# Attention's projections and layer 0's gate and up products: seven float32 products of sums, or three float32r passes over split operands

## The chip, the cores and the metric

The kernel runs on one core of a Trainium2 chip. The metric is the device time of one execution in microseconds (us), as the median of several runs; lower is better. The profile speaks of engines: PE is TensorE's matrix products and PEld its weight loads, DVE is VectorE, ACT is ScalarE, POOL is GpSimd, and SP is the engine that issues most of the transfers. [...]

## What is computed

Two transformer layers over 4 sequences of 256 tokens with 256 features, float32, with a layer norm after each of four sublayers:

```python
x = layernorm(x + L0_attn(x))   # 16 heads, 128 plain + 64 rotary features each, values of 128
x = layernorm(x + L0_ffn(x))    # silu(x W1^T) * (x W3^T), a Walsh-Hadamard transform, W2
x = layernorm(x + L1_attn(x))   # mLSTM with 8 heads, then a gated MLP of its own
x = layernorm(x + L1_ffn(x))    # gated MLP with int8 weights and scales

# L0_attn
q, k, v = x @ Wq.T, x @ Wk.T, x @ Wv.T
scores = q_nope k_nope / sqrt(128) + rope(q_rope) rope(k_rope) / sqrt(64)
out = (softmax(scores) @ v).reshape(...) @ Wo.T
```

## The kernel before

**Blocks of attention.** Heads are taken by pairs p (8 pairs), tokens by halves n (512 tokens, two sequences). One block h = 2p + n holds the scores and softmax of pair p and half n, and three other things that fill TensorE meanwhile: the projections of block h + 1, the weighted values of block h - 1 (steps V00 to V11), and the output products of block h - 1 (O0, O1), which are added to `acc[n]`. There are 16 blocks. The order of TensorE's instructions in a block is written out by hand (`ORDER`, and `EARLY` for the first two); `in_turn` chains each product behind the last. All engines run their own instructions strictly in the built order; what stands on VectorE, GpSimd or the transfer queue behind a waiting instruction waits too. `behind(x)` makes an instruction come after x.

**Scores and softmax.** `scores` makes the plain products (L455) into four PSUM banks, two with the tag `sc` and two with `pt`, and the rotary ones (L467) on top. `maxima` (L478, DVE), `exponentials` (L487, ACT), `normalized` (L495 and L497, DVE) and `block_transposed` (L505, DVE) follow for each sequence and head; `finish(k)` is normalisation and block transposition of one of the four. `spread` (L512) then completes the transposition with 16 transfers from SP's queue into `prT`, and the next block's V steps wait for all of these.

**Projections.** For the first block they are plain float32 products (`projections`). For the others `fast_projections` uses a Winograd form of Strassen's scheme: each pair of 2x2 blocks (256 input features in two halves, 512 tokens in two sequences) takes seven products of sums of blocks instead of eight. The sums of the weights (`weight_sums`, L285 to L288, DVE) are made once a pair, those of the input (`input_sums`) once a half. There are four groups: rotary (3), plain queries (0), plain keys (1), values (2); steps A1 to A7 take groups 3 and 0 in banks `mm`, steps B1 to B7 groups 1 and 2 in banks `sc`. Rotary products are scaled, added, then turned: `turn` exchanges neighbouring partitions (`stream_shuffle`, L312, DVE) and GpSimd multiplies by cosine and sine and adds (L315 to L317, three instructions of 128x512 for queries and three for keys). The shuffle of blocks after the first is held behind the last normalisation of the softmax:

```python
with behind(settled["softmax"]) if h > 1 else contextlib.nullcontext():
    nc.vector.stream_shuffle(swp, raw[c], SWAP)
```

**PSUM.** A tag is a ring of two banks of 512 columns: `mm`, `sc`, `pt`, `ot`. A product that starts a bank waits until the bank's last reader is done.

**Layer 0's feed-forward.** `ffn0(0)` uses the same seven products (`fast_glu`), `ffn0(1)` plain float32 products of 512 columns (`glu`). The Walsh-Hadamard transform is folded into W2: butterflies on GpSimd (L678, L679) during attention, and four products with `had` (L687), two in the last block and two ahead of the feed-forward. `ffn0(1)` is interleaved with mLSTM of half 0 by `merge`, which gives the second stream so many us of TensorE work for each wait of the first; so it goes on with `ffn1(0)` and mLSTM of half 1. Layer norms and RMS norms (`layernorm`, `rmsnorm`, with `rsqrt` in 13 small DVE instructions) are taken over four token tiles at a time.

**Layer 1's feed-forward** already uses float32r: a float32 input is split into a rounded part and the rest, and each meets the int8 weights, which need no splitting, in one product of one pass (L1279 with 512 columns, L1329 with 256).

Of the kernel before, what the change touches and what calls it, by code (L numbers as in the profile page):

```python
# [17 lines left out]
P = 128  # L18
# [17 lines left out]
SWAP = [i ^ 1 for i in range(32)]  # L36


@with_exitstack
def tile_two_layers(ctx: ExitStack, tc: tile.TileContext, a: dict, out: bass.AP):  # L40
# [10 lines left out]
    def rsqrt(v, n, scale, eps):  # L51

        ve = small.tile([P, n], F32, tag="rs_v", name="rs_v")
        nc.vector.tensor_scalar(ve, v, scale, eps, ALU.mult, ALU.add)
        sh = small.tile([P, n], I32, tag="rs_sh", name="rs_sh")
# [20 lines left out]
    xT = attn.tile([P, KC, NT], F32, tag="xT", name="xT", bufs=1)  # L76
# [16 lines left out]
    def load_pair(p):  # L93

        w = attn.tile([P, KC, 3 * 384], F32, tag="w", name="w_qkv", bufs=2)
        if p == 0:
            for i in range(KC):
                nc.sync.dma_start(w[:, i, 0:256], a["w_qkv"][p][:, i, 0:256])
            for lo, hi in ((256, 384), (640, 768), (384, 640)):
                nc.sync.dma_start(w[:, :, lo:hi], a["w_qkv"][p][:, :, lo:hi])  # L100
            load_tables()
            nc.sync.dma_start(w[:, :, 768:1024], a["w_qkv"][p][:, :, 768:])
            nc.sync.dma_start(cst[:, 512:1024], a["cst"][:, 640:1152])
        else:
            nc.sync.dma_start(w[:, :, 0:1024], a["w_qkv"][p])
        wr = attn.tile([P, KC, 2, P], F32, tag="wr", name="w_rot")
        if p != 1:
            turned_weights(w, wr)
        return w, wr

    def turned_weights(w, wr):

        for i in range(KC):
            for k in range(2):
                nc.gpsimd.tensor_copy(
                    wr[:, i, k, :].rearrange("p (h f x) -> p h f x", h=2, x=2),
                    w[:, i, 256 + 384 * k : 384 + 384 * k].rearrange("p (h x f) -> p h f x", h=2, x=2),
                )

# [7 lines left out]
    weights = {0: load_pair(0)}  # L127
    nc.sync.dma_start(xT[:, :, HALF:], a["xT"][:, :, HALF:])
# [5 lines left out]
    weights[1], w_os[1] = load_pair(1), load_output(1)  # L134
# [4 lines left out]
    def ff_weight(name, engine=nc.sync, dtype=F32):  # L139

        tiled = [P, NH, D] if name in ("w2", "w_down", "q_down") else [P, KC, FF]
        t = wts.tile(tiled, dtype, tag="ff", name=name, bufs=7)
# [4 lines left out]
    pair_sums = lambda k: wts.tile([P, 4, 4 * P], F32, tag="ff", name=f"wsum{k}", bufs=7)  # L147
    wsums = [pair_sums(0)]
    xsum = wts.tile([P, 2, 4, S], F32, tag="ff", name="xsum", bufs=7)
    wsums.append(pair_sums(1))  # L150
    w2b = wts.tile([P, NH, D], F32, tag="ff", name="w2b", bufs=7)
    w2, w1, w3 = (ff_weight(k) for k in ("w2", "w1", "w3"))

# [11 lines left out]
    def hidden_sums(engine, ws, which, to=None):  # L165


        for x, w in enumerate(ws):
            part = lambda i, c: w[:, i, :].rearrange("p (k c d) -> p k c d", c=2, d=P)[:, :, c, :]
            one, two = gsum[:, 0, x], gsum[:, 1, x]  # L170
            if which == "first":
                engine.tensor_tensor(one, part(0, 1), part(1, 1), ALU.add)
                last = engine.tensor_tensor(two, one, part(0, 0), ALU.subtract)
            elif which == "third":
                last = engine.tensor_tensor(gsum3[:, x], part(0, 0), part(0, 1), ALU.subtract)
            else:
                last = engine.tensor_tensor(to[:, x] if to else part(0, 1), part(1, 0), two, ALU.subtract)
        return last

    def projections(h):  # L180
# [3 lines left out]
        w, wr = weights[p]  # L184
# [80 lines left out]
    def input_sums(n):  # L265
        tok = lambda b: slice((2 * n + b) * S, (2 * n + b + 1) * S)
        one, two, three, four = (xsum[:, n, m, :] for m in range(4))
        nc.vector.tensor_tensor(one, xT[:, 0, tok(1)], xT[:, 0, tok(0)], ALU.subtract)
        nc.vector.tensor_tensor(two, xT[:, 1, tok(1)], one, ALU.subtract)
        nc.vector.tensor_tensor(three, xT[:, 1, tok(1)], xT[:, 0, tok(1)], ALU.subtract)  # L270
        return nc.vector.tensor_tensor(four, xT[:, 1, tok(0)], two, ALU.subtract)

    def weight_sums(p, groups=((0, 3), (3, 4))):


        w, wr = weights[p]
        sums = wsums[p % 2]
        for g0, g1 in groups:
            if g0 == 3:
                part = lambda i, c: wr[:, i, c, :]  # L280
                at = lambda m: sums[:, m, 384:512]
            else:
                part = lambda i, c: w[:, i, :].rearrange("p (g c x) -> p g c x", g=3, c=3)[:, g0:g1, c, :]
                at = lambda m: sums[:, m, 0:384].rearrange("p (g x) -> p g x", g=3)[:, g0:g1, :]
            nc.vector.tensor_tensor(at(0), part(0, 1), part(1, 1), ALU.add)  # L285
            nc.vector.tensor_tensor(at(1), at(0), part(0, 0), ALU.subtract)
            nc.vector.tensor_tensor(at(2), part(0, 0), part(0, 1), ALU.subtract)
            last = nc.vector.tensor_tensor(at(3), part(1, 0), at(1), ALU.subtract)  # L288
        return last

    def fast_projections(h):

        p, n = divmod(h, 2)
        w, wr = weights[p]
# [5 lines left out]
        batch = lambda b: slice(b * S, (b + 1) * S)  # L300
        raw = []

        def rotary(c, b):
            if not raw:
                raw.extend(attn.tile([P, HALF], F32, tag="raw", name="rope_raw", bufs=3) for _ in range(2))
            return raw[c][:, batch(b)]

        def turn(c):

            swp = attn.tile([P, HALF], F32, tag="swp", name="rope_swp", bufs=3)  # L310
            with behind(settled["softmax"]) if h > 1 else contextlib.nullcontext():
                nc.vector.stream_shuffle(swp, raw[c], SWAP)  # L312
            by_b = lambda t: t.rearrange("p (b s) -> p b s", s=S)
            cs, sn = (t.unsqueeze(1).to_broadcast([P, 2, S]) for t in (cos, sin))
            nc.gpsimd.tensor_tensor(by_b(raw[c]), by_b(raw[c]), cs, ALU.mult)  # L315
            nc.gpsimd.tensor_tensor(by_b(swp), by_b(swp), sn, ALU.mult)  # L316
            rotated[h] = nc.gpsimd.tensor_tensor((qr, kr)[c], raw[c], swp, ALU.add)  # L317

        def group(which):

            at = (0, 384, 768, None)[which]
            if which == 3:
                block = lambda c, i: wr[:, i, c, :]
            else:
                block = lambda c, i: w[:, i, at + c * P : at + (c + 1) * P]
            dst = (
                lambda c, b: qn[:, c, batch(b)],
                lambda c, b: kn[:, c, batch(b)],
                lambda c, b: v[:, 2 * b : 2 * b + 2, c * P : (c + 1) * P],
                rotary,  # L330
            )[which]
            scales = ((QSCALE, QSCALE), (1.0, 1.0), (1.0, 1.0), (RSCALE, 1.0))[which]
            return which, block, dst, scales

        def factors(g, m):
            which, block = g[0], g[1]
# [13 lines left out]
        def pair_of_groups(tag, which):  # L350
# [3 lines left out]
            def products(name, m, start):  # L354
                if start and name not in found:
                    found[name] = bank(tag)
# [1049 lines left out]
    for c in (2, 3):  # L1406
        hadamard(c)
# [135 lines left out]
```

## Time and profile before

| | |
|---|---|
| Runs (us) | 694.88, 694.0, 696.69; median 694.88 |
| Profiled execution: span | 692.4 us from the first to the last instruction; its own time is not listed apart from the runs, whose median is 2.5 us above the span |
| Engines busy | PE 680.3 us (98%), DVE 474.0 (68%), ACT 280.2 (40%), POOL 183.0 (26%) |
| Granted TensorE clock | 0.997 of full speed |
| Attention blocks 2 to 14 | start 24.68 us apart, at 63.0 to 383.8 us |
| Layer 0's feed-forward, first half | products from 410 to 437 us |
| Layer 1's int8 feed-forward | from 638 us to the end |

A row of the profile names the line, the engine, the operation, the tile written and the tiles read, and the shape. In a group, "busy" is the sum, then comes the mean of one in ns. In a timeline, the first two numbers are start and duration in us, "x8" merges eight instructions in a row, and a bracket tells how long the engine had been idle and who released it. One float32 product appears as two PE records. Records of PE include the pipeline's fill and drain, so the time that a product takes of TensorE is the distance from start to start.

### The profile page before, as it was taken

To read this page: it belongs to the slowest core of one execution; us is meant where nothing else is said; L and a number is where in the kernel's file an instruction comes from. 1 tells how busy PE (TensorE), PEld (TensorE's weight loads), DVE (VectorE), ACT (ScalarE), POOL (GpSimd) and SP (SyncE) were. 2 spreads that over 40 slices of the span, in tenths; PEclk is the share of its full clock that TensorE was granted. 3 is DMA by queue.
4 is the path that set the end of the run, shared out by engine and by line. 5 is a ranking of instruction groups with operands and counts; after the bars stand their busy time and mean duration, and the time that the engine had idled before them with its cause. 6 is when DMAs were issued, how large, how long until landed. Compare 5 with 4: busy or idle time off the path is not lost.

```text
span 692.4 us, 10218 instructions
## 1 busy us (share of the span) xinstructions
PE 680.3 (98%) x3504; PEld 551.4 (80%) x3504; DVE 474.0 (68%) x1310; ACT 280.2 (40%) x839; POOL 183.0 (26%) x191
## 2 busy tenths in 40 slices
PE   9999999999999999999999999999999999999995
PEld 5888988988888898898888878845685568788785
DVE  5966766666477478467747786474779648966767
ACT  2442543344254254334425355136412561261652
POOL 3254314413431440441442920004100140000210
PEclk9999999999999999999999999999999999999998
DMA  8543233232331421520331322003031300001001
GB/s 270 216 123 61 39 100 62 54 95 51 67 96 36 108 66 26 138 57 17 64 62 28 96 47 87 1 0 124 1 121 62 120 4 1 0 1 62 0 1 62
DMA packets 49030, 45.46 MB, mean 66 GB/s; under 512 B 9521, under 2 KB 42705, under 8 KB 47825
## 3 DMA queue, kind: packets, MB, share of 16 engines
q1 hardware_dynamic: 48112, 41.00, 22.8%
q0 software_dynamic: 432, 3.15, 1.3%
q10 hardware_dynamic: 432, 0.66, 0.3%
q8 instruction: 28, 0.46, 0.3%
q14 instruction: 26, 0.20, 0.1%
HBM read 25.61 MB, written 1.08 MB: 39 GB/s over the span
## 4 chain that ended last, share of the span: by engine, by line
PE 88%; DVE 8%; ACT 2%; POOL 1%; issue 1%; DVEq 0%; ACTq 0%
PE ps_mm L371 13%; PE ps_mm L70 10%; PE ps_ot L70 8%; PE ps_d L70 7%; PE ps_sc L363 6%; PE ps_sc L371 6%; PE ps_d L930 4%; PE ps_d L1279 4%; PE ps_m L70 4%; PE ps_sc L455 4%; PE ps_pt L455 4%; PE ps_m L871 4%; PE ps_d L871 3%; PE ps_sc L467 2%; PE ps_m L930 2%; PE ps_m L1195 2%
## 5 line engine op out<-in xcount | busy, mean ns | idle before, releaser
L315 POOL TENSOR_TENSOR rope_raw<-rope_raw,cst 128x512 f32<-128x512 f32 x30 | 38.2, 1272 | 181.8 <-DVE rope_swp L312 181.8
L487 ACT ACTIVATE pr<-ps_sc,nmax 128x256 f32<-128x256 f32 x64 | 29.7, 475 | 121.3 <-DVE nmax L478 121.3
L70 PE MATMUL ps_mm<-w_o,oT 128*128 128x256 f32 x256 | 62.2, 379 | 0.0
L70 PE MATMUL ps_ot<-prT,v 128*128 128x256 f32 x240 | 61.4, 380 | 0.1
L569 DVE TENSOR_TENSOR acc<-ps_mm,acc 128x512 f32<-128x512 f32 x32 | 22.1, 690 | 48.3 <-PE ps_mm L70 48.3
L70 PEld LDWEIGHTS ps_mm<-w_o,oT 128*128 128x128 f32 x256 | 46.6, 190 | 5.3
L70 PEld LDWEIGHTS ps_ot<-prT,v 128*128 128x128 f32 x240 | 43.3, 190 | 5.5 <-issue 0.8
L1153 POOL TENSOR_TENSOR ex<-cst,ex 128x512 f32<-128x512 f32 x16 | 19.7, 1266 | 93.7 <-DMA ex<-far 93.7
L385 ACT COPY kn<-ps_sc 128x256 f32<-128x256 f32 x56 | 20.9, 373 | 58.3 <-PE ps_sc L363 58.2
L497 DVE TENSOR_SCALAR pr<-pr,rinv 128x256 f32<-128x256 f32 x128 | 42.8, 375 | 1.6
L371 PE MATMUL ps_mm<-xsum,wsum 128*128 128x256 f32 x180 | 43.9, 380 | 0.0
L505 DVE STREAM_TRANSPOSE cross<-pr 128x512 f32<-128x512 f32 x60 | 42.6, 711 | 1.4
L478 DVE TENSOR_REDUCE nmax<-ps_sc 128x2 f32<-128x512 f32 x32 | 20.6, 686 | 32.7 <-PE ps_sc L467 32.6
L316 POOL TENSOR_TENSOR rope_swp<-rope_swp,cst 128x512 f32<-128x512 f32 x30 | 38.1, 1270 | 0.0
L371 PEld LDWEIGHTS ps_mm<-xsum,wsum 128*128 128x128 f32 x180 | 33.9, 190 | 4.5
L394 DVE TENSOR_TENSOR kn<-ps_sc,kn 128x256 f32<-128x256 f32 x42 | 17.8, 423 | 28.5 <-ACT kn L385 18.1
L487 ACT ACTIVATE pr<-ps_pt,nmax 128x256 f32<-128x256 f32 x64 | 30.1, 489 | 2.6 <-DVE nmax L478 2.6
L455 PE MATMUL ps_sc<-kn,qn 128*128 128x256 f32 x128 | 30.2, 379 | 0.0
L455 PE MATMUL ps_pt<-kn,qn 128*128 128x256 f32 x128 | 30.2, 379 | 0.0
L70 PE MATMUL ps_d<-fm,w 128*128 128x512 f32 x64 | 29.4, 599 | 0.0
L930 PE MATMUL ps_d<-w,hT 128*128 128x256 f32 x128 | 28.4, 379 | 0.0
L363 PEld LDWEIGHTS ps_sc<-wsum,xsum 128*128 128x128 f32 x168 | 25.4, 191 | 2.2
(317 smaller groups left out, 1631.0 us busy)
## 6 DMA issues: line engine op xcount, KB each, us to landing
prT<-cross SPq DMA_DIRECT2D x240, 64.0 KB, 2.1
w_qkv<-in_w_qkv SPq DMA_DIRECT2D x7, 1024.0 KB, 7.0
ex<-far SPq DMA_DIRECT2D x8, 512.0 KB, 5.1
w<-in_w SPq DMA_DIRECT2D x3, 1024.0 KB, 11.6
w_o<-in_w_o SPq DMA_DIRECT2D x8, 256.0 KB, 3.3
acc<-in_x SPq DMA_DIRECT2D x2, 512.0 KB, 9.0
w_up<-in_w_up SPq DMA_DIRECT2D x1, 1024.0 KB, 4.9
w_gate<-in_w_gate SPq DMA_DIRECT2D x1, 1024.0 KB
```

The source lines that it names most:

```text
L70: last = nc.tensor.matmul(ps, lhsT=lhs(i), rhs=rhs(i), start=(i == 0), stop=(i == n - 1))
L315: nc.gpsimd.tensor_tensor(by_b(raw[c]), by_b(raw[c]), cs, ALU.mult)
L316: nc.gpsimd.tensor_tensor(by_b(swp), by_b(swp), sn, ALU.mult)
L363: lambda: nc.tensor.matmul(ps[:, k * S + j * P : k * S + (j + 1) * P], lhsT=x[:, j * P : (j + 1) * P], rhs=wt, start=(start and not k and ...
L371: lambda: nc.tensor.matmul(ps[:, k * S : (k + 1) * S], lhsT=wt, rhs=x, start=(start and not k), stop=True, skip_group_check=True,)
L455: lambda: nc.tensor.matmul(ps[bb][e][:, qt * S : (qt + 1) * S], lhsT=qn[:, e, queries(bb, qt)], rhs=kn[:, e, keys(bb)], start=(qt == 0), s ...
L487: nc.scalar.activation(pr[:, qt, :], ps[:, qt * S : (qt + 1) * S], AF.Exp, bias=nmax[:, qt : qt + 1], accum_out=rsum[:, qt : qt + 1],)
L497: nc.vector.tensor_scalar(pr[:, qt, :], pr[:, qt, :], rinv[:, qt : qt + 1], None, ALU.mult)
L505: return nc.vector.transpose(cross[:, :, e], pr.rearrange("p t (x i) -> p x t i", i=32))
L871: nc.tensor.matmul(banks[name][:, batch(x)], lhsT=left, rhs=right, start=start and not x, stop=True, skip_group_check=True,)
L930: lambda: nc.tensor.matmul(po, lhsT=hT[:, i, j * P : (j + 1) * P], rhs=wd[:, i, :], start=(i == 0), stop=(i == NH - 1),)
L1279: nc.tensor.matmul(ps, lhsT=lhs, rhs=rhs, start=(k == 0), stop=(k == len(terms) - 1))
```

## The change

**Three passes.** Each float32 operand of the projections is written as the sum of a high part of 12 significant bits (the low 12 bits masked off) and the rest. With high parts H, h and rests L, l, the product is found from three one-pass float32r products of prepared operands, with the scale 2^-12 (`STEP`): two kinds are summed in one PSUM bank, the third in another, and a result is bank 0 times (1 + 2^-12), minus bank 1. So each group of 128 output features takes 6 products of 512 columns and fills two banks; ScalarE copies the first with the scale, VectorE subtracts the second (`joined`). Values take 24 products of 256 columns a block. `ffn0` uses the same for both halves (`split_glu`, 12 products of 512 columns for each pair of gate and up tiles).

**Splitting.** `split` masks on DVE, subtracts on POOL (or DVE for inputs), joins mask and rest on DVE, and copies on ACT. A pair's weights have four parts, R (rotary), Q, K and W (values), split one pair ahead: R, Q and K in even blocks after steps Q0, K0 and W0, W in odd blocks after R1. `weight_sums`, `input_sums` and the Strassen sums of layer 0's feed-forward go.

**Order.** The blocks have a new `ORDER`; the rotary groups come first, in banks `mm` and `sc`, and the shuffle is no longer held behind the softmax. Blocks 0 and 1 use `ot` in place of `sc`.

**Memory and loads.** The parts, the Strassen sums that stay (layer 1's MLP, half 1), and the feed-forward weights share named slots; one buffer instead of two takes a pair's raw weights; w1 and w3 are loaded near the end of attention and split there (`hidden_parts`); w_gate and w_up load after layer 0's gate and up. The Hadamard products move into blocks 12 and 13. Layer 1's int8 parts lie in quarters.

**Norms by pairs.** The norm ahead of mLSTM is joined with the layer norm before it, from the same statistics, for two token tiles at a time right after their rows are done (`mlstm_rows`); the norm ahead of layer 1's MLP goes by pairs too (`mlp_rows`). The waits that `merge` is given change with it.

The diff, cut to its core:

```diff
-            nc.sync.dma_start(w[:, :, 0:1024], a["w_qkv"][p])
+            nc.sync.dma_start(w, a["w_qkv"][p])          # bufs=1 instead of 2
...
+    def split(src, to, top, scaled, engine=nc.gpsimd, views=None, fine=nc.vector):
+        if views is None:
+            views = [(src, top, to[1])]
+        for x, t, low in views:
+            nc.vector.tensor_single_scalar(t.bitcast(I32), x.bitcast(I32), TOP, ALU.bitwise_and)
+        for x, t, low in views:
+            engine.tensor_tensor(low, x, t, ALU.subtract)
+        low = to[1].bitcast(F32)
+        if scaled:
+            nc.scalar.mul(to[1], low, 1.0 / STEP)
+            last = nc.vector.tensor_tensor(to[2], top, low, ALU.subtract)
+        elif fine is nc.gpsimd:
+            nc.scalar.mul(to[2], top, STEP)
+            last = nc.gpsimd.tensor_tensor(to[2], to[2].bitcast(F32), low, ALU.subtract)
+        else:
+            last = nc.vector.scalar_tensor_tensor(to[2], top, STEP, low, ALU.mult, ALU.subtract)
+        nc.scalar.copy(to[0], top)
+        return last
...
+        def passes(ps, left, right, first=True):
+            for at, ks in ((0, (0, 1)), (1, (2,))):
+                terms = [(k, i) for i in range(KC) for k in ks]
+                for m, (k, i) in enumerate(terms):
+                    in_turn(lambda: nc.tensor.matmul(ps[at], lhsT=left(k, i), rhs=right(k, i), ...))
+        def joined(dst, ps, scale):
+            copied = nc.scalar.mul(dst, ps[0], scale * (1.0 + STEP))
+            if scale == 1.0:
+                return copied, nc.vector.tensor_tensor(dst, dst, ps[1], ALU.subtract)
+            return copied, nc.vector.scalar_tensor_tensor(dst, ps[1], -scale, dst, ALU.mult, ALU.add)
...
-            with behind(settled["softmax"]) if h > 1 else contextlib.nullcontext():
-                nc.vector.stream_shuffle(swp, raw[c], SWAP)
+            nc.vector.stream_shuffle(swp, raw, SWAP)
...
-    ORDER = "A1 A2 V00 A6 V01 A7 A5 B1 B2 A3 A4 B6 B7 V10 B5 V11 O0 B3 O0 B4 O1 O1".split()
+    ORDER = "R0 V00 V01 R1 V10 Q0 V11 O0 O0 Q1 K0 K1 O1 O1 W0 W1".split()
+    SPLITS = ({"Q0": "R", "K0": "Q", "W0": "K"}, {"R1": "W"})
...
+            elif step == "R1":
+                with behind(done):
+                    finish(1)
+                with behind(copied):
+                    found.append(exponentials(ps[1][1], top[3]))
+            elif step == "Q0":
+                with behind(done):
+                    finish(2)
+            elif step == "Q1":
+                with behind(done):
+                    settled["softmax"] = finish(3)
                 out = spread(crossed)
+            name, ahead = SPLITS[h % 2].get(step), h // 2 + 1
+            if name and ahead < NPAIR:
+                with behind(settled["softmax"] if step[0] in "KW" else done):
+                    pair_part(ahead, name)
...
+    def split_glu(x, wg, wu, hT, tag, smooth):
+        for c in range(NH):
+            pg, pu = [bank(tag) for _ in range(2)], [bank(tag) for _ in range(2)]
+            fill(lambda: three_products(pg, wg, x, c))
+            yield 1.35
+            fill(lambda: three_products(pu, wu, x, c))
...
+    def mlstm_rows(n, j):
+        ...
+        nc.vector.tensor_scalar(ve[:, 0:2], mv[:, :, 1], 1.0 + RMS_EPS, RMS_EPS * LN_EPS, ALU.mult, ALU.add)
+        nc.vector.tensor_scalar(ve[:, 2:4], mv[:, :, 1], LN_EPS, None, ALU.add)
+        y = root(ve, 4)
```

## The prediction

> **What bounds the kernel now.** First the page: how busy each engine is, and which engine carries the chain that ended last.
>
> ```profile
> PE 680.3 (98%) x3504; PEld 551.4 (80%) x3504; DVE 474.0 (68%) x1310; ACT 280.2 (40%) x839; POOL 183.0 (26%) x191
> ...
> PE 88%; DVE 8%; ACT 2%; POOL 1%; issue 1%; DVEq 0%; ACTq 0%
> ```
>
> TensorE is the bound over nearly the whole span. Second, the table by stretches, for 13 equal attention blocks, 63.0 to 383.8 us (columns: length, then busy us of PE, PEld, DVE, ACT, POOL):
>
> ```profile
> 63.00:383.80 320.80, 320.80 (x1743) 280.92 (x1742) 213.65 (x546) 130.40 (x442) 106.62 (x102) 1.00 0.29 64
> ```
>
> A block takes 320.8 / 13 = 24.68 us, VectorE works 16.4 us of it, GpSimd 8.2. Third, the chain in order of time through one block shows no engine but PE, so nothing but TensorE work sets a block's length:
>
> ```profile
> 309.94 1.73 PE ps_sc L455 x8
> 311.66 1.73 PE ps_pt L455 x8
> 313.39 1.06 PE ps_sc L467 x8
> 314.45 0.86 PE ps_pt L467 x8
> 315.32 0.84 PE ps_mm L371 x3
> ```
>
> Fourth, the timeline, for what a float32r product costs and for what VectorE and GpSimd do to each other:
>
> ```profile
> 649.31 1.07 PE L1279 MATMUL ps_d<-qx,q_gate 128*128 128x512 f32 x4
> 650.22 1.07 PE L1279 MATMUL ps_d<-qx,q_up 128*128 128x512 f32 x4
> ...
> 673.12 11.67 PE L1329 MATMUL ps_m<-q_down,qh 128*128 128x256 f32 x96
> ```
> ```profile
> 14.46 1.46 POOL L205 TENSOR_TENSOR rope_raw<-rope_raw,cst 128x512 f32<-128x512 f32 x1
> 15.88 1.44 POOL L207 TENSOR_TENSOR qr<-rope_raw,rope_swp 128x512 f32<-128x512 f32 x1
> ```
> ```profile
> 14.72 1.48 DVE L270 TENSOR_TENSOR xsum<-xT 128x256 f32<-128x256 f32 x1
> 16.12 1.48 DVE L269 TENSOR_TENSOR xsum<-xT,xsum 128x256 f32<-128x256 f32 x1
> ...
> 299.87 0.35 DVE L497 TENSOR_SCALAR pr<-pr,rinv 128x256 f32<-128x256 f32 x1
> ...
> 388.76 1.66 DVE L497 TENSOR_SCALAR pr<-pr,rinv 128x256 f32<-128x256 f32 x2
> ```
> ```profile
> 300.99 10.28 SPq L512 DMA_DIRECT2D prT<-cross  x16
> ```
>
> Four 512-column float32r products start 0.91 us apart, 0.227 each; 256 columns: (11.67 - 0.28) / 95 = 0.120. The add of two SBUF tiles, 0.42 us where GpSimd rests, takes 1.48 us beside GpSimd and ends just after GpSimd's instruction. The normalisation (L497) takes 0.35 us alone; the pair at 388.76 takes 1.66 beside GpSimd. All 8 normalisations that overlap GpSimd took 0.62 to 0.93. The other 120 miss GpSimd, because the code holds the rotary shuffle, and so GpSimd's rope, behind the softmax. Adds that read PSUM are unchanged beside GpSimd (0.42).
>
> **TensorE's saving.** A float32 product is two records, 0.216 us each at 256 columns (32 in 7.07 us, L930), 0.111 at 128, 0.43 at 512 (a gate's four start 1.72 us before the next). A block's projections are now 42 records of 256 columns and 28 of 128: 9.07 + 3.11 = 12.18 us. After: six feature groups of 6 products at 0.227 and 24 value products at 0.120: 8.17 + 2.88 = 11.05. That is 1.13 less, 17.0 over 15 blocks. Layer 0's gate and up: the first half falls from 112 records (24.2) to 96 products (21.8), the second from 64 records of 512 (27.5) to 21.8: 8.1 less. Together 25.1 us, if nothing else becomes late.
>
> [...]
>
> **What takes the saving away.** The built order shows two changes on the in-order queues. The rotary shuffles are no longer held back, so GpSimd's six rope products (1.23 us from start to start) run through the middle of each softmax. And each weight part is masked on VectorE, subtracted on GpSimd behind these ropes (1.23 a part; R in four strided pieces, 0.41 each estimated from the 256-column 0.69 of L678), and then joined on VectorE (0.61), which waits for GpSimd. Three parts fall in even blocks, one in odd. Queued behind that wait are the PSUM drains that free TensorE's banks: each feature group fills two banks, and the second is freed only by VectorE.
>
> I walk a block from the start of R0 (zero), with start-to-start times: maximum, drain, accumulation 0.61, transposition 0.64, shuffle 0.62, normalisation 0.27, reciprocal 0.18; the block is 24.68 - 1.13 = 23.55 without stalls.
>
> Common part: the maxima end at 1.7 as now, R0's drain at 3.1, its transposition and shuffle at 4.4; GpSimd ropes from 4.5.
>
> Even block, counting only the order: GpSimd ends six ropes at 11.8 and R's four pieces at 13.5; VectorE, at R's join by 10.8, waits and ends it at 14.1, Q1's drain at 14.7. K1's second bank was due at 12.9: 1.85 lost. Later O1's row add stands behind Q's join (behind GpSimd) and K's mask: 19.9, where W0's second bank was due at 17.9: 2.05 lost. Sum 27.45. With the waits beside GpSimd: the second head's normalisations start at 6.2 and end at 8.5 instead of 6.8, the third's end at 12.6; O0's row add ends at 14.4, where K0's second bank was due at 11.5 (3.0 lost), and O1's at 21.1 against 19.0 (2.1 lost). Sum 28.65.
>
> Odd block: by order alone W's join ends at 10.1 and the drain of Q0 at 11.3, against 10.6 for K0's bank; O0's add costs another 0.4: 24.7. With the waits Q0's drain ends at 13.2 (2.6 lost) and O0's add at 15.45 against 14.15 (1.3 lost): 27.5.
>
> So a block is 26.1 by order alone and 28.1 with the waits: 1.4 to 3.4 more than now. I take 3.0, near the upper end, since every overlapped row shows the wait, and somewhat below, as no row shows whether the masks wait too. Thirteen blocks (h = 2 to 14): +39, from +18 to +44.
>
> [...]
>
> Opening: VectorE's queue now has the join of Q, the input masks, the value copies and the joins of K and W ahead of the first maxima. GpSimd's subtraction of Q stands between the ropes, so the second shuffle starts at 18.3, not 12.93; ropes end at 22.1, K's and W's pieces at 26.0, the maxima begin near 26.6, not 23.7: +2.9 by order, +6.7 with the waits. Blocks 0 and 1 have the same stalls, and R0 for h = 2 waits for the second half's input parts (two masks, two subtractions, two joins, about 3.3 us, after the value drains). I take +8 for all of it, from +5 to +16.
>
> End of attention: eight masks and four joins (5.3 us) join 20.4 us of VectorE work in 26.2 us, with 12 subtractions on GpSimd where the butterflies were: 0 to +6, I take +3. The butterflies and Hadamard products move into blocks 5 to 13 at equal work.
>
> Layer 0's feed-forward: -8.1 on TensorE; the first half's tokens must be copied, masked, subtracted and scaled ahead of its products, about 2.5 us that the Hadamard products used to cover: -5.6. VectorE has 1.83 us to do per 2.72 us of TensorE there, so this saving should hold; if mLSTM's chain lacks filler in the second half, -3.
>
> Norms by pairs: the gaps at the norms are 0.2 to 0.9 us, some 2 us in all, and VectorE hides the rest: 0 (at most -2). The feed-forward weights now load when their slots come free, with 13.8 us of down products as cover: 0; without it a 1 MB load of 4.9 us would show.
>
> Sum: 39 + 8 + 3 - 5.6 = +44.4, a span of 736.8. The profiled execution spans 692.4, the median of the runs is 694.9, so 2.5 lies around it: 739 us.
>
> **Rivals.** [...] (2) TensorE keeps the bound: if each second bank is drained before it is due, which needs Q1's drain by 12.9 and O1's row add by 17.9 in even blocks, 692.4 - 25.1 + 2.5 = 669.8, so 672 us, faster. For it: VectorE's own work, about 17.3 us a block, fits into 23.5, and PE is 98% busy now. Against: R's pieces stand behind 7.4 us of ropes on a queue that keeps its order. (3) The transfers of the probabilities: the last transposition ends near 18.5, sixteen issues and the landing take 9.6 + 2.1, so the next V00 can start at 30.2, while an odd block asks for it at 28.9; if this adds 1.3 us to each block instead of overlapping the stalls, 756 us.
>
> **Numbers.** Forecast 0.58, order alone 0.17, transfers 0.05, TensorE's saving kept 0.16, about cancelled 0.04. A measurement of this kernel can tell about 0.5% from no change. Slower 0.80, same 0.04, faster 0.16. The range takes in the order-alone case with some block stalls fewer (703) up to the walk's upper ends (760), and leaves out rival 2.
>
> **What would show it.** Right: blocks of 27 to 29 us, alternating; PE below 95% busy; PE in the blocks waiting for DVE drains and row adds; L438's normalisations mostly above 0.6 us; DVE waiting for POOL at the joins. Wrong: blocks near 23.5, PE still 98% busy, and normalisations at 0.35.

## The result and the profile after

The changed kernel takes 793.86 us (median of four runs, 788.75 to 794.81), the kernel before, measured with it, 695.79 (694.0 to 697.01): a ratio of 1.140, 95% interval 1.136 to 1.144. The forecast was 739 us, between 703 and 760. The side was right, the loss was 98 us where 44 were expected. Times and ratios here are of runs at a like clock: one run of the kernel with two kinds of products (808.12 us, mean granted clock 0.926 against 0.948 to 0.961) is left out.

The page of the profile after, its busy times, the row of the granted clock, and the chain that ended last; then the clock row of the kernel before:

```profile
PE 703.4 (89%) x3370; PEld 551.9 (70%) x3370; DVE 567.0 (72%) x1312; ACT 312.3 (39%) x763; POOL 247.9 (31%) x235
...
PEclk9899999999979989989999998999999999999999
...
PE 49%; DVE 25%; POOL 9%; SPq 6%; issue 5%; ACT 4%; DMA 2%; DVEq 0%; POOLq 0%; ACTq 0%
```
```profile
PEclk9999999999999999999999999999999999999998
```

Two things are to be read here. TensorE carries 49% of the chain, not 88%. And it is busy 23 us longer although it was given 25 us less to do: its records got longer. The clock row says most of why. It has a seven and four eights, where the one before has a single eight, at the very end; the mean granted clock fell from 0.997 to 0.947.

The stretches of the span, cut at the same products in both kernels (us; blocks are cut at their first plain score):

| stretch | before | after | difference | forecast |
|---|---|---|---|---|
| start to block 2 | 63.0 | 84.5 | +21.5 | +8 |
| blocks 2 to 14 | 320.8 | 392.1 | +71.3 | +39 |
| block 15 to the first gate product | 26.2 | 32.9 | +6.7 | +5.5 (3 and 2.5 for the input's split) |
| layer 0's feed-forward, first half | 39.7 | 38.1 | -1.6 | -2.4 |
| its second half, beside mLSTM | 74.2 | 77.2 | +3.0 | -5.7 |
| up to layer 1's seven products, second half | 75.5 | 74.1 | -1.4 | 0 |
| the rest | 93.0 | 93.4 | +0.4 | 0 |

The table by stretches for the thirteen blocks together and for blocks 4, 5 and 6 alone (columns: length, then busy us of PE, PEld, DVE, ACT, POOL, then the granted clock):

```profile
84.50:476.60 392.10, 341.62 (x1622) 276.39 (x1621) 274.02 (x512) 140.18 (x367) 155.93 (x146) 0.93 0.25 57
...
142.30:171.20 28.90, 24.45 (x127) 19.92 (x126) 22.00 (x43) 11.16 (x30) 12.23 (x12) 1.00 0.20 39
171.20:200.00 28.80, 25.80 (x126) 21.09 (x125) 19.93 (x37) 10.04 (x28) 9.55 (x7) 0.94 0.31 81
200.00:233.90 33.90, 27.30 (x126) 21.93 (x125) 22.73 (x43) 11.17 (x30) 17.61 (x20) 0.85 0.17 33
```

The blocks are 33.3 (block 1), then 28.9 four times, 33.9, 30.1, 33.9, 28.9, 34.6, 27.9, 30.9, 30.6 and 25.8 us. Three kinds matter: the even block of 28.9 us at full clock (2 and 4), as the walk had it (28.65); the odd block of 28.9 (3, 5 and 9), where the walk had 27.5, with TensorE busy longer at a lower clock; and blocks 6, 8 and 10, 5 us longer than any walk.

**The waits**, from the groups: normalisations beside GpSimd, and joins that wait for it (columns: busy, mean ns, idle before).

```profile
L438 DVE TENSOR_SCALAR pr<-pr,rinv 128x256 f32<-128x256 f32 x128 | 80.6, 671 | 1.3
...
L142 DVE SCALAR_TENSOR_TENSOR wp<-top,wp 128x512 fp32r<-128x512 f32 x32 | 30.6, 959 | 37.9 <-POOL wp L133 37.9
```

The normalisations' mean was 375 ns. The joins wait 37.9 us for GpSimd in all.

**The odd block.** TensorE's timeline in block 5, then the table by stretches, cut into pieces of 3.41 us on the grid on which the clock changes: one piece of block 4 for comparison, and three in a row of block 5. The number behind the five busy times is the granted clock.

```profile
189.51 1.20 PE L323 MATMUL ps_mm<-xp,wp 128*128 128x512 f32 x4 [1.89 <-DVE qn L332]
191.82 0.94 PE L323 MATMUL ps_mm<-xp,wp 128*128 128x512 f32 x2 [1.11 <-DVE acc L510]
192.55 2.76 PE L323 MATMUL ps_sc<-xp,wp 128*128 128x512 f32 x6
```
```profile
158.04:161.45 3.41, 1.63 (x8) 0.98 (x6) 3.41 (x8) 0.00 (x0) 2.92 (x4) 1.00 0.00 0
188.76:192.17 3.41, 1.55 (x6) 0.98 (x7) 3.38 (x7) 0.60 (x1) 1.91 (x2) 1.00 0.56 231
192.17:195.58 3.41, 3.41 (x10) 2.64 (x9) 2.84 (x8) 0.60 (x1) 0.00 (x0) 0.50 0.00 0
195.58:199.00 3.42, 3.42 (x24) 3.21 (x23) 1.35 (x3) 0.60 (x1) 0.00 (x0) 1.00 0.46 89
```

Both waits are in the walk: Q0's drain and O0's row add free K0's two banks late. What follows is not: six products that need 1.5 us at full clock (1.54 in a later run below) take 2.76, at a granted clock of 0.50, while nothing waits any more. The stall is paid a second time. In the piece ahead of the drop TensorE was busy for 1.55 of 3.41 us. Over the whole span the clock is at 0.50 in 18 such stretches of one, two or three pieces on one grid (the last is cut off by the end of the span), 84.8 us together, with TensorE busy in 69.1 of them.

**Block 6**, GpSimd's, VectorE's and TensorE's rows:

```profile
217.79 0.77 POOL L586 TENSOR_TENSOR w2b<-w 128x256 f32<-128x256 f32 x1
...
220.61 0.48 POOL L133 TENSOR_TENSOR wp<-w_qkv,top 128x128 fp32r<-128x128 f32 x1
...
225.19 0.69 DVE L142 SCALAR_TENSOR_TENSOR wp<-top,wp 128x512 fp32r<-128x512 f32 x1 [4.55 <-POOL wp L133]
225.80 0.68 DVE L332 SCALAR_TENSOR_TENSOR qn<-ps_sc,qn 128x512 f32<-128x512 f32 x1
...
226.54 1.22 PE L323 MATMUL ps_sc<-xp,wp 128*128 128x512 f32 x2 [2.91 <-DVE qn L332]
```

The butterflies (L586, L587: eight of 0.72 to 0.77 us in each of blocks 6, 8 and 10) stand in GpSimd's queue behind the last rope, four ahead of R's four subtractions and four between them. R's join waits 4.55 us behind them, Q1's drain behind the join, K1's second bank behind the drain.

### The profile page after: what moved, and what is told of

The parts are those of the page before. It is cut to its first block, busy times and chain, and to the rows that moved or that the text cites. A ratio compares the mean times of both kernels' runs of the same rounds, so it can differ in the third digit from the quotient of the medians.

```text
span 792.3 us, 10065 instructions
## 1 busy us (share of the span) xinstructions
PE 703.4 (89%) x3370; PEld 551.9 (70%) x3370; DVE 567.0 (72%) x1312; ACT 312.3 (39%) x763; POOL 247.9 (31%) x235
## 4 chain that ended last, share of the span: by engine, by line
PE 49%; DVE 25%; POOL 9%; SPq 6%; issue 5%; ACT 4%; DMA 2%; DVEq 0%; POOLq 0%; ACTq 0%
SPq L453 6%; DVE pr L438 5%; PE ps_mm L76 4%; PE ps_d L741 4%; PE ps_d L76 4%; PE ps_d L1322 3%; PE ps_ot L76 3%; PE ps_sc L323 3%; POOL wp L133 3%; PE ps_mm L323 3%; PE ps_m L899 3%; PE ps_pt L396 2%; PE ps_d L958 2%; PE ps_sc L396 2%; DVE cross L446 2%
## 5 line engine op out<-in xcount | busy, mean ns | idle before, releaser
L323 PE MATMUL ps_mm<-xp,wp 128*128 128x512 f32 x270 | 83.2, 434 | 40.2 <-DVE acc L510 25.0
L323 PEld LDWEIGHTS ps_mm<-xp,wp 128*128 128x128 f32 x270 | 49.4, 195 | 63.7 <-DVE acc L510 30.9
L323 PE MATMUL ps_sc<-xp,wp 128*128 128x512 f32 x234 | 76.8, 467 | 8.0 <-DVE qn L332 8.0
L438 DVE TENSOR_SCALAR pr<-pr,rinv 128x256 f32<-128x256 f32 x128 | 80.6, 671 | 1.3
L323 PEld LDWEIGHTS ps_sc<-xp,wp 128*128 128x128 f32 x234 | 50.0, 217 | 22.5 <-DVE qn L332 11.0
L133 POOL TENSOR_TENSOR wp<-w_qkv,top 128x128 fp32r<-128x128 f32 (+1 forms) x56 | 46.3, 833 | 44.1 <-DVE top L131 43.8
L142 DVE SCALAR_TENSOR_TENSOR wp<-top,wp 128x512 fp32r<-128x512 f32 x32 | 30.6, 959 | 37.9 <-POOL wp L133 37.9
L364 PE MATMUL ps_mm<-wp,xp 128*128 128x256 f32 x180 | 30.0, 312 | 8.1 <-DVE acc L510 5.0
L364 PEld LDWEIGHTS ps_mm<-wp,xp 128*128 128x128 f32 x180 | 25.5, 198 | 10.6 <-DVE acc L510 6.0
L131 DVE TENSOR_SCALAR top<-w_qkv 128x128 int32<-128x128 int32 (+1 forms) x56 | 27.6, 508 | 6.0 <-DMA w_qkv<-in_w_qkv 5.9
L396 PE MATMUL ps_sc<-kn,qn 128*128 128x256 f32 x128 | 31.5, 390 | 0.0
```

What stands on the lines that cost most here:

```text
L133: engine.tensor_tensor(low, x, t, ALU.subtract)
L142: last = nc.vector.scalar_tensor_tensor(to[2], top, STEP, low, ALU.mult, ALU.subtract)
L323: lambda: nc.tensor.matmul(ps[at], lhsT=left(k, i), rhs=right(k, i), start=(m == 0), stop=(m == len(terms) - 1))
L364: lambda: nc.tensor.matmul(ps[at][:, t * S : (t + 1) * S], lhsT=xp[k][:, i, j * P : (j + 1) * P], rhs=part[:, k, i, :], start=(m == 0), st ...
L396: lambda: nc.tensor.matmul(ps[bb][e][:, qt * S : (qt + 1) * S], lhsT=qn[:, e, queries(bb, qt)], rhs=kn[:, e, keys(bb)], start=(qt == 0), s ...
L438: nc.vector.tensor_scalar(pr[:, qt, :], pr[:, qt, :], rinv[:, qt : qt + 1], None, ALU.mult)
```

## The experiments

In the blocks, the lost time could come from four things: VectorE waiting beside GpSimd, VectorE waiting for GpSimd's queue, the butterflies, and the clock. The first four kernels are the changed kernel with one or two of these taken away.

**Ropes back behind the softmax.** `rotary` no longer turns its result; the shuffle and the three GpSimd instructions are kept as a closure and run after `finish(3)`:

```diff
-            nc.vector.stream_shuffle(swp, raw, SWAP)
+            held.append(lambda: turning(c, raw))   # shuffle behind settled["softmax"], then the ropes
```

> The rotary shuffles, and with them GpSimd's six ropes, are put back behind the softmax. Own theory (three things add up in the blocks: VectorE's waits beside GpSimd, its waits for GpSimd's subtractions behind the ropes, and a lower granted clock after each stall): normalisations fall from a mean of 671 ns to about 350, R's subtraction no longer stands behind ropes, but Q's and K's do; blocks 2 to 14 average about 26.5 us instead of 30.2, granted clock up from 0.947 to about 0.97, 740 us (720 to 765). [...] Rival 2, the queue behind the ropes is all: the wait only moves from R's join to Q's and K's, 785 to 800 us.

Measured: 752.02 us, ratio 1.082 (1.079 to 1.086). Blocks 2 to 14 average 26.57 us, the clock is 0.966.

**The weights' subtractions on VectorE.**

```diff
-        return split(..., to, top, False, views=views)
+        return split(..., to, top, False, nc.vector, views=views)
```

> The subtractions of the weight parts go from GpSimd to VectorE (about 0.6 us each, R's four pieces some 1 us), so VectorE waits for nothing that GpSimd makes; the ropes stay in the softmax. Own theory: the joins' waits for GpSimd (37.9 us idle before L142 in TensorE's view) go, the normalisations beside GpSimd stay long (mean above 550 ns), blocks average about 27, butterflies no longer delay a join; granted clock about 0.97; 745 us (725 to 770). [...] Rival 2 (queue is all): blocks near 24, 690 to 710.

Measured: 781.92 us, ratio 1.125 (1.122 to 1.129); blocks average 29.55, blocks 6, 8 and 10 still 33.5 to 35.7. This is 12 us above my own range.

**Both.**

> Both edits together. Own theory: no rope beside the softmax, no VectorE instruction behind GpSimd's queue; VectorE's own work is about 18 us of a block of 23.5, so the blocks come near TensorE's limit, 23.7 to 24.5 us, granted clock above 0.99 there, opening some us shorter; 695 us (680 to 715). If instead something else binds the blocks (the transfers of the probabilities, VectorE's order of drains), they stay above 26 and the time above 730.

Measured: 732.10 us, ratio 1.053 (1.050 to 1.056); blocks average 25.53, clock 0.981. Groups of the three kernels, in this order: normalisations and joins with the ropes held, normalisations with VectorE's subtractions, normalisations with both.

```profile
L444 DVE TENSOR_SCALAR pr<-pr,rinv 128x256 f32<-128x256 f32 x128 | 51.0, 440 | 1.6
L142 DVE SCALAR_TENSOR_TENSOR wp<-top,wp 128x512 fp32r<-128x512 f32 x32 | 31.7, 992 | 37.0 <-POOL wp L133 37.0
```
```profile
L438 DVE TENSOR_SCALAR pr<-pr,rinv 128x256 f32<-128x256 f32 x128 | 69.9, 587 | 0.9
```
```profile
L444 DVE TENSOR_SCALAR pr<-pr,rinv 128x256 f32<-128x256 f32 x128 | 45.9, 401 | 1.6
```

Against 793.9, the first edit gives 41.9 us, the second 12.0, both 61.8. Holding the ropes leaves the joins' wait for GpSimd as it was (37.0 us) and still wins most: the place of the ropes is worth over three times the queue behind them. It does two things at once, since R's subtraction then also stands ahead of the ropes. My own figures for the second and third kernel were too good by some 37 us each: removing a wait for GpSimd is worth little while its ropes still hold up the same instructions.

**Butterflies into odd blocks**, behind W's subtraction:

```diff
-            with tc.issue_after(rotated[{1: 7, 2: 9, 4: 11}[h]].ins):
+            with tc.issue_after(settled[{1: 5, 2: 7, 4: 9}[h]].ins):   # the subtraction of W in blocks 5, 7, 9
```

> The 24 butterfly instructions on GpSimd (8 of 0.72 us in each of the even blocks 6, 8 and 10, there between R's pieces) go into the odd blocks 5, 7 and 9, behind the subtraction of W; nothing else changes. Own theory: blocks 6, 8 and 10 (33.9, 33.8, 34.6 us) fall to the 28.9 of blocks 2 and 4, blocks 5, 7 and 9 gain at most 1 us each; 793.9 - 15 + 2 = 781 us (776 to 786). Rival (butterflies are hidden, those blocks are longer for another reason): 794, no change.

Measured: 776.63 us, ratio 1.118 (1.115 to 1.121). Blocks 6, 8 and 10 are 29.2 us; the thirteen blocks take 16.5 us less. The place of 24 instructions of 0.72 us was worth 15 to 17 us (by the ratios, and by the times). Most of it comes by way of the clock: in the thirteen blocks TensorE's idle time falls from 50.5 to 44.5 us, its busy time from 341.6 to 331.1, and the part of this at half speed from 46.4 to 22.6; the mean granted clock of the span rises from 0.947 to 0.972.

**The kernel before, its shuffles not held.** If the hold was what kept ropes and normalisations apart before, lifting it alone must show:

```diff
-            with behind(settled["softmax"]) if h > 1 else contextlib.nullcontext():
-                nc.vector.stream_shuffle(swp, raw[c], SWAP)
+            nc.vector.stream_shuffle(swp, raw[c], SWAP)
```

> The kernel before with one edit: its rotary shuffles are not held behind the softmax any more, so that GpSimd's ropes run beside the normalisations; nothing of the three passes or the splitting is in it. Own theory: normalisations rise from a mean of 375 ns to 550 or more, but VectorE works only 16.4 us of a block of 24.68 and waits for nothing from GpSimd, so the blocks grow by 0.3 to 1.0 us: 700 to 708 us. Rival (ropes beside the softmax alone explain the changed kernel's blocks): blocks of 27 us or more, 725 or above. Rival (VectorE's slack hides all of it): 693 to 697.

Measured: 695.29 us, ratio 1.0008 (0.9998 to 1.0018): nothing. Its normalisations:

```profile
L496 DVE TENSOR_SCALAR pr<-pr,rinv 128x256 f32<-128x256 f32 x128 | 42.5, 374 | 1.6
```

They lie no more beside GpSimd than they did. In the old order the rotary products end so late in the block that the ropes run behind the softmax anyway: in block 4 they start at 128.1 us without the hold and at 129.0 with it, and the last pair of normalisations starts at 126.8 (126.9 with the hold). It is the new order, R0 and R1 first, that moved the ropes.

**TensorE's stalls filled** with products nobody reads, into a free `pt` bank (in the first of the two kernels also in even blocks; the text on record says K1 there, it was K0's second bank):

```diff
+        def extra(count):
+            if count and h > 2:
+                ps = bank("pt")
+                for m in range(count):
+                    in_turn(lambda: nc.tensor.matmul(ps, lhsT=xp[0][:, 0, 0:P], rhs=xp[0][:, 0, tok], ...))
...
             for at, ks in ((0, (0, 1)), (1, (2,))):
+                extra(more[at])      # odd blocks: 6 and 3 ahead of K0's two banks
```

> The changed kernel with extra one-pass products of 512 columns (0.227 us each at full clock, their results unused) put in TensorE's order where it stands still: even blocks 6 before K1's second bank is not yet free and odd blocks 6 before K0's first and 3 before its second bank, 5 before W0's second bank in even blocks; about 30 us more work for TensorE in all. Own theory (a stall lowers the granted clock for the next microseconds, and that half speed is part of the loss): granted clock up from 0.947 to 0.97 or more, odd blocks from 28.9 to 27.5, and the time falls by 10 to 25 us in spite of the added work, 770 to 785 us. Rival 1 (the stalls alone set the pace, the half speed hides in them): 790 to 798. Rival 2 (the added work is itself late): 800 to 825.

> As the kernel with filled stalls, but only in odd blocks: 9 extra one-pass products of 512 columns in each (2.0 us more work for TensorE), in the two places where it stands still for 1.9 and 1.1 us; even blocks as in the changed kernel. Own theory (a stall is paid twice, the second time as products at half clock): odd blocks fall from 28.9 to 27.3 as they did with all stalls filled, so the whole kernel gets faster by doing more: 793.9 - 6 x 1.6 = 784 us (780 to 789). Rival (the clock's drop hides in later waits): 792 to 798.

Measured: with all stalls filled 800.15 us, with those of odd blocks alone 788.88 us, ratio 1.135 (1.131 to 1.138); the first missed my range by 15 us. In both, blocks 5, 7, 9 and 11 take 27.2 to 27.3 us, block 5 instead of 28.9. TensorE's timeline in block 5 of the second kernel, and the block's stretch:

```profile
187.22 1.54 PE L323 MATMUL ps_pt<-xp 128*128 128x512 f32 x6
189.29 1.20 PE L335 MATMUL ps_mm<-xp,wp 128*128 128x512 f32 x4 [0.53 <-DVE qn L344]
190.32 0.84 PE L323 MATMUL ps_pt<-xp 128*128 128x512 f32 x3
191.61 0.73 PE L335 MATMUL ps_mm<-xp,wp 128*128 128x512 f32 x2 [0.44 <-DVE acc L524]
192.18 1.54 PE L335 MATMUL ps_sc<-xp,wp 128*128 128x512 f32 x6
```
```profile
170.90:198.30 27.40, 26.43 (x136) 21.78 (x135) 20.00 (x37) 10.19 (x28) 9.58 (x7) 1.00 0.33 82
```

Nine products more, and the block is 1.6 us shorter: the six products of `ps_sc` take 1.54 us, not 2.76, and the clock stays at 1.00. So half speed after a stall is a cost of its own, here 1.6 us a block. In even blocks the extra products made it worse (block 4 takes 30.7 us): there the clock was at 1.00 already, and VectorE's order came out different; what of this costs the 1.8 us was not separated. The whole kernel gained 4 us by the ratios (the intervals just overlap), not the 9.6 of six odd blocks, because other blocks moved up (block 12 is 32.4 us).

**The softmax earlier.** As with both edits, the normalisations one step earlier: `finish(1)` behind R0, `finish(2)` behind R1, `finish(3)` behind Q0.

> As with both edits (shuffles behind the softmax, subtractions of the weights on VectorE), and the last three normalisations one step earlier in the order (behind the joins of R0, R1 and Q0 instead of R1, Q0 and Q1), so that ropes and transfers start about 3 us earlier. Own theory: what is left of the blocks' loss (25.5 us against 24.68) is TensorE waiting for ropes that end after the plain scores of the next block (0.8 us in odd blocks), so the blocks fall to about 24.3, and block 15 starts its values sooner: 732 - 16 - 3 = 713 us (705 to 722). Rival (VectorE's order is the limit, and drains now stand behind the normalisations): no gain, 728 to 740.

Measured: 766.62 us, ratio 1.105 (1.101 to 1.108). Wrong by 54 us. But odd blocks take 23.7 us, and only even ones went up, to 31.5 and more (block 14 to 30.1). GpSimd's, VectorE's and TensorE's rows in an even block:

```profile
148.75 1.30 POOL L356 TENSOR_TENSOR rope_raw<-rope_raw,cst 128x512 f32<-128x512 f32 x1 [14.52 <-DVE rope_swp L353]
...
151.29 4.10 DVE L133 TENSOR_TENSOR wp<-w_qkv,top 128x128 fp32r<-128x128 f32 x4
...
155.31 0.68 DVE L516 TENSOR_TENSOR acc<-ps_mm,acc 128x512 f32<-128x512 f32 x1
...
156.04 1.22 PE L324 MATMUL ps_mm<-xp,wp 128*128 128x512 f32 x2 [5.52 <-DVE acc L516]
```

The earlier ropes now lie beside R's split. Four small subtractions take 4.10 us, while GpSimd's ropes, 1.27 to 1.40 us each, run one after another. O0's row add stands behind them.

**The split of the input's first half at the very start**, on top of that:

> As the kernel with the early softmax, and the split of the input's first half goes from behind block 0 to the very start, where VectorE is idle (0.9 and 2.7 us busy in the second and third 5 us of the span). Own theory: R0 of block 1 waited up to 7.6 us for this split, so block 1 falls by 6 to 8 us and the opening moves by less than 1.5 us: 707 us (700 to 714). Rival (block 1 is long because of the drains and joins of VectorE): 713, no change.

Measured: 766.61 us, where the kernel with the early softmax took 766.62: no change.

**Splits placed away from the ropes**, as in the early softmax kernel otherwise:

```diff
-    SPLITS = ({"Q0": "R", "K0": "Q", "W0": "K"}, {"R1": "W"})
+    SPLITS = ({"W0": "Q", "W1": "K"}, {"R1": "W"})
...
+            if step == "O0" and settled["out"] is not None:      # even blocks
+                with behind(settled["out"]):
+                    pair_part(h // 2 + 1, "R")
+            if step == ("Q0" if h % 2 else "Q1"):                 # shuffles and ropes only now
+                while held:
+                    held.pop(0)()
```

> As the kernel with the early softmax, with the splits of even blocks taken away from the ropes: R's split stands behind O0's row add and ahead of the rotary shuffles (so GpSimd rests meanwhile), Q's and K's behind the joins of the values at the block's end. In the early softmax kernel R's four strided subtractions took 4.10 us beside the ropes, about 1.0 each, and O0's row add behind them freed K0's second bank 5.5 us late. Own theory (a VectorE instruction beside GpSimd waits for it, and what stands behind it frees TensorE's banks): R's pieces fall to about 0.25 each, the wait of 5.5 us goes, odd blocks stay at 23.7, even ones come to 24.0 to 24.8: 766.6 - 13 x 4.2 = 712 us (704 to 722), blocks shorter than the 24.68 of the kernel before, the rest of the loss then in the opening and the end. Rival (VectorE has too much work in even blocks wherever it stands): even blocks above 27, 735 or more.

Measured: 721.49 us, ratio 1.038 (1.035 to 1.041). The same rows, and two blocks:

```profile
141.87 0.69 DVE L516 TENSOR_TENSOR acc<-ps_mm,acc 128x512 f32<-128x512 f32 x1 [0.25 <-PE ps_mm L76]
...
143.02 0.90 DVE L133 TENSOR_TENSOR wp<-w_qkv,top 128x128 fp32r<-128x128 f32 x4
```
```profile
126.80:150.50 23.70, 23.70 (x126) 20.15 (x126) 18.15 (x44) 10.08 (x28) 5.77 (x5) 1.00 0.27 52
150.50:175.10 24.60, 24.17 (x126) 19.96 (x125) 21.73 (x43) 10.99 (x30) 9.74 (x9) 1.00 0.34 90
```

The four subtractions take 0.90 us instead of 4.10, and the even block falls from 31.5 to 23.7, TensorE busy without a gap. This is the limit that the walk started from (23.55). VectorE does the same work as in the early softmax kernel, in another order; the run moved R's, Q's and K's splits together, so what each of them was worth is not separated.

**Layer 0's second half with two kinds of products.**

```diff
+            pg, pu = [bank(tag)] * 2, [bank(tag)] * 2     # second half: no products into a second bank
```

> The changed kernel, but layer 0's feed-forward leaves out the third kind of products in its second half, the one that runs beside mLSTM (8 instead of 12 products for each pair of gate and up tiles: 32 products of 0.227 us less, 7.3 us of TensorE; joins as before, on the first bank). Own theory (that stage is bound by mLSTM's chain of small steps, which lacks filler once the products get cheaper): it falls by less than 3 us from 77.2, total 790 to 795 us. Rival (TensorE still bounds the stage, and the added joins or the granted clock of 0.98 took the expected gain): it falls by 6 us or more, total 785 to 788.

Measured: 789.44 us (788.98 to 791.21), ratio 1.137 (1.133 to 1.140), that is 2.5 us less than the changed kernel by the ratios, with overlapping intervals. 7.3 us of TensorE's work were taken away, and most of it did not come back. That mLSTM's chain bounds the stage is likely by this but not shown: the stage's own length was not compared, and in the changed kernel TensorE is busy for 71.7 of its 77.2 us.

**Everything moved at once.**

```diff
+                    with tc.issue_after(rotated[3 + count // 3].ins):   # butterflies three at a time
...
+    with behind(settled["norm"]):          # the last normalisation of block 15
+        hidden_parts(0)
+        hidden_parts(1)
```

> As the kernel with placed splits (odd blocks 24.6, even ones 23.7, but 26.5 in blocks 7, 9 and 11, beside whose softmax GpSimd makes the butterflies), with three more moves: the butterflies three at a time behind the ropes of blocks 2 to 9; the split of the input's first half at the very start (R0 of block 1 and with it block 1's rotary scores waited for it, 46.1 to 56.1 us); at the end of attention the splits of w1 and w3 behind the last softmax, not ahead of its maxima. Own theory: blocks 7, 9 and 11 fall to 24.6 (-5.7), block 1 from 32.3 to about 28 (-4), the end by 3 (a wait of 4.6 us for the weighted values' copy goes): 721.5 - 12.7 = 709 us (704 to 714), still over 1% slower than the kernel before, since opening and end remain some 20 us longer and TensorE's saving in 13 blocks is 13 or less. Rival (the saving of the three passes can be had in full once the waits are gone): 685 to 695.

Measured: 718.74 us, ratio 1.035 (1.032 to 1.038). Block 1 fell to 28.0, as expected, but the time missed the range by 5 us. The odd blocks 3 to 9 are all 26.0 now: the butterflies' cost was spread, not removed. And what follows block 15's start takes 321.7 us, 3 more than with the placed splits. This is the lowest time that was found, though its interval overlaps that of the placed splits. Against the kernel before, 10.9 us of its loss lie ahead of block 2 (73.9 to 63.0), 1.1 in the thirteen blocks (24.76 a block), and 13.1 after them.

**One part for seven in the opening.**

> The changed kernel with the splitting of seven weight parts left out in the opening: only R of pair 0 is split, and Q, K and W of pair 0 and all four parts of pair 1 use its parts again (the products run as before, on other numbers); the input's two halves are still split. From block 2 on it does the same work as the changed kernel. Own theory (the opening's 21.5 us come from the split work on VectorE and GpSimd and from the ropes' and drains' waits for it, with the granted clock's drop behind them): block 2 starts at 70 to 75 us instead of 84.5 (63.0 in the kernel before), the time falls by 9 to 14 us, 780 to 785 us. Rival (the opening is long for the ropes beside the softmax and for the input's split, not for the weights'): block 2 starts at 80 or later, 789 us or more.

Measured: 779.41 us, ratio 1.123 (1.118 to 1.129); block 2 starts at 69.9 us. The split work of seven weight parts, with the waits for it, costs 14.6 of the opening's 21.5 us.

## Why the prediction was right in its side and wrong in its size

**TensorE's saving: right in the blocks.** Where nothing waits, a block is 23.7 us, 0.98 less than before; the sum had 1.13.

**The waits in the blocks: right in kind, and for even blocks in size.** The walk gave 28.65 with the waits, and 28.9 was measured; the same waits stand in the trace (K0's second bank freed late by O0's row add, W0's by O1's). "I take 3.0" of a possible 3.4, since no row showed whether masks wait too, was the wrong end: R's masks wait as well (four of 128 columns took 0.64 us alone with the placed splits; two took 2.17 beside the ropes in the early softmax kernel, one 1.16 in the changed kernel).

**The step that failed** is the term of 39 us for the thirteen blocks, which measured 71.3. Two costs are missing from it, and they overlap.

- "The butterflies and Hadamard products move into blocks 5 to 13 at equal work." A price of nothing must name its cover, and none was named. GpSimd was free where they went, but VectorE's join stood behind them: 5 us in each of three blocks, and moving them gave 16.5 us of the blocks back. Blocks 12 and 13, with two Hadamard products each, are 2 us longer than their like; 1.7 us of it is the products themselves, which the kernel before did behind block 14, so some 3.4 us of the 71.3 are only moved.
- The granted clock. The walk added up the time that TensorE stands still and let it run on at full speed. The waits it named for the odd block came true (27.3 us with the clock kept up, 27.5 forecast), the block took 28.9. The sum holds 25.1 us of saved work and a span 44.4 longer, so it implied some 69 us more idle time. TensorE's idle time rose by 77 us (88.9 against 12.1): this was nearly right, in part by luck, since some 6 us of it came with the butterflies. The rest of the error is in its busy time: 48 us above the 655.2 that the sum implies. TensorE was busy for 69.1 us at a granted clock of 0.50; if that work took half as long at 1.00, about 34 of the 48 are the clock (an estimate). In the thirteen blocks it is 46.4 us, so by the same estimate about 23 of the 32 us by which the term was off; their idle time was 50.5 us where the sum implied 53.7.

What the changed kernel's trace shows of the clock is two values, 1.00 and 0.50, which change on a grid of 3.41 us. Block 5 has no idle time as long as a piece of it, but waits of 1.89 and 1.11 us, and the piece ahead of the drop was busy 45%. Block 4, with waits of 2.49 and 1.96 us five microseconds apart, keeps 1.00: the grid cuts the longer wait in two, and its least busy piece was busy 48%. The profile before has 0.50 in its last 4.8 us alone, and the prediction has no term for it.

**The opening: mis-sized,** 21.5 for 8. The sum counted the wait for the first maxima and added little for blocks 0 and 1. Each of the three parts lost 6 to 8 us (block 0 starts at 26.9, not 19.0; it takes 24.3, not 18.2; block 1 33.3, not 25.9), since seven weight parts and both halves of the input are split within the first 60 us, ahead of the drains. Leaving out the work of seven parts gave 14.6 us back; what makes up the rest was not tested. One row each of the opening and of block 15:

```profile
47.96 0.74 PE L364 MATMUL ps_mm<-wp,xp 128*128 128x256 f32 x4 [3.02 <-ACT v L329]
...
485.12 3.75 PE L76 MATMUL ps_ot<-prT,v 128*128 128x256 f32 x8 [5.59 <-DMA prT<-cross]
```

**The end of attention: near** (6.7 for 5.5), with another cause: the second row is the third rival, the transfers of the probabilities, which cost 5.59 us once, at block 15, and hardly anywhere else.

**Layer 0's feed-forward: wrong in its second half.** The fall-back "if mLSTM's chain lacks filler" (-3) came nearer and was still too good: 3.0 us were lost there, and taking away 7.3 us more work gave about 2.5, not clear of noise. The cause stays open.

**A reason that was wrong.** The prediction said that normalisations miss GpSimd "because the code holds the rotary shuffle". Lifting the hold alone changes nothing. The effect was forecast rightly, from the built order, but laid to the wrong line. Nor did the other 120 all miss GpSimd: twelve of them ran beside its copies of 128x128 (0.31 to 0.43 us each) and took 0.31 to 0.41, so not every overlapped row shows a long wait.

**The rivals.** Order alone does not stand: the kernel whose VectorE waits for no result of GpSimd, but keeps the ropes beside the softmax, is still 12.5% slower, with 33.5 to 35.7 us in the blocks with the butterflies. TensorE keeping the bound is what the kernel with placed splits shows in its even blocks; its condition, drains before they are due, was not met by the order as written.

## What to carry to other kernels

Where one engine is busy 98% of the time, work taken from it is worth nothing if the work that prepares it lands on engines whose order frees its buffers; walk those queues, and give every moved instruction a price on each queue, that of an engine "with room" too. A stall like the one in block 5, which left TensorE busy for 1.55 of 3.41 us, is to be booked twice, once as waiting and once as half speed afterwards (1.6 us of that block). Before such a change is given up, move the preparing work between the drains: with the same products and the same splits, but the weights' subtractions on VectorE and another order, the time fell from 794 to 719 us here, though not below 695.

## What the runs showed of the hardware that was not expected

- In the changed kernel's trace half speed comes in whole pieces of 3.41 us on one grid (the end of the span cuts the last), and follows how busy TensorE was in the piece before: all 15 pieces at full clock in which it was busy 45% or less were followed by one at 0.50, three of the four at 48 to 52% were, and none at 54% or more. In block 5 two stalls of 1.89 and 1.11 us were enough; added products in the gaps kept the clock there at 1.00 and shortened the block by 1.6 us.
- A subtraction of two SBUF tiles on VectorE took longer beside GpSimd's ropes: the four of 128x128 took 4.10 us together in the kernel with the early softmax (ropes of 1.27 to 1.40 us), and 0.90 alone with the placed splits. In the changed kernel, one of 128x512 took 1.75 us beside a rope (two records) and 0.68 to 0.69 alone (six). So four small pieces cost more there than one large. Masks of 128x128 waited too: in the changed kernel the seven that started beside a rope took 1.16 to 1.34 us and ended 0.08 to 0.09 after it, where one alone took 0.22.
